# Attention stores one per slot, a weight stream resumed in one go, and two kinds of work moved between engines

## The chip, the cores and the metric

The kernel runs on one core of a Trainium2 chip. The metric is the device time of one launch in microseconds (us). The profile is one further execution, recorded by the hardware profiler; its engines are TensorE (PE, with its weight loads PEld), VectorE (DVE), ScalarE (ACT), GpSimd (POOL) and SyncE (SP), the last of which here issues nearly all transfers between DRAM and the on-chip memory.

## The reference, cut to what matters

The input `x` holds 128 graphs of 64 tokens with 768 features, `adj` a 0/1 matrix per graph. A layer norm and a relu come first, then two attention layers over each graph, then a residual sum:

```python
h = relu(layernorm(x))
for l in range(2):
    m_left, m_right = h @ W_left[l].T, h @ W_right[l].T
    u_left  = einsum('bih,bjh->bij', h, m_left)  / sqrt(768)
    u_right = einsum('bih,bjh->bij', h, m_right) / sqrt(768)
    u = u_left above and on the diagonal, u_right below it      # by triu/tril of adj
    e = exp(u) * adj
    attention = e / (e.sum(-1) + 1e-10)
    ctx = attention @ (h @ W_lin[l].T + b_lin[l])
    h = relu((ctx - mean(ctx)) / (std(ctx, ddof=1) + 1e-3) * a[l] + b[l])
out = x + h
```

## The kernel before, in words

**Passes.** The 8192 tokens are cut into 16 blocks of 512 (8 graphs each), and two blocks make a superblock `U`; there are 8 superblocks. For each layer, `pass_one` (L447) computes the projections m_left and m_right, the scores and the softmax, and stores the attention weights to DRAM (`ATT`). `pass_two` computes the linear layer, applies the attention (`context`) and the norm, and writes the next layer's rows (or the output).

**Products.** A projection is done with a scheme of fast matrix multiplication: `PRODUCTS` lists 29 products, each of a weight tile (a 256x256 block or a sum of blocks, `W_OPS`) and a token tile (a block or a sum, `X_OPS`), whose results are added into the outputs with signs. Each product is made twice, with the left weights (kind 0, into banks X, Y, Z) and the right ones (kind 1, into bank V and two banks `right`), 8 matmuls each, in `project` (L526, the matmul is L538). `read` copies or adds a finished bank into `m`; the additions are DVE's (L221 is the helper `added` that all sums go through). The token sums (`ts`) are GpSimd's. `pass_two`'s `linear` (matmul L1042) uses a similar scheme of 15 products (`ORDER`) over the blocks X, Z, Y, V: its first product writes X, its second (i=1) Z, and its sixth (i=5) is the first to write V.

**Order of the work.** The order is written out by hand. Each product has four slots (0.86 us of PE each), 116 per superblock. `put(slot, f)` hangs work on a slot, `put_all(slot, fs, step)` a list of it, and `run(slot)` (called between matmuls) issues what hangs there. A second list, `idle`, gives up one entry in each slot on which nothing hangs; what is left of it at the end of `pass_one` is issued at once (L763). This decides the order on each engine's queue[...].

**Scores.** The scores of the two blocks of the superblock before are computed after products 0 and 2 (`TURNS`, `scores`, L481, 192 short matmuls). Each block then has a softmax `chain` (L485 to L518): masks times adjacency on GpSimd (`wm`, L489), four DVE reads of the scores' bank (L495), a sum (L499), the exponential on ACT, the normalisation on DVE (L503 to L509), a DVE transpose (L513), and 8 stores to `ATT` (L518). It is a generator; `softmax(u)` is a list of 8 steps of it. The last two blocks have no superblock after them: after the leftover idle work, `pass_one` fills bank X with the bias, computes both scores, the last one's into bank V (L769), runs the chain of block 14 at once, and hangs that of block 15 on slots of `pass_two`.

**Weights.** In the first superblock of layer 0 (`first`, L569) the weight sums are made from the raw weights while the products run: left sums on DVE, right ones (kind "r") on GpSimd for products 2 to 8 and on DVE otherwise (L652). `keep_weight` (L193) stores every product's weights to DRAM (`WS`), and `Singles` hands out the tiles for the sums; a tile is used again once its store has landed. All later superblocks stream the 29 weight pairs from DRAM into a ring of 8 tiles `RING` (`stream`, L196; `wp<-ws` in the profile), the next one being issued after each product (`streamed`, L562). `HELD` (L523) says after which products the stream lags behind: by up to 4 tiles at products 0 and 1, and back by one each at 2, 3, 4 and 5. In `first` the first three streams of the second superblock are issued after product 25 and four more after product 28 (L697 to L702).

**Blocks.** While one superblock is projected, the next one's two blocks are prepared (`block`, L728): `load_rows` (8 loads), `transpose_rows` (L384: in layer 0 the layer norm's statistics and its normalisation on ACT, in both layers four DVE transposes), a `store` of four transfers to `KEPT` (`h<-room`), later `load_h` (`ht<-h`). The statistics of blocks 2 and 3 (`u < 4`) in layer 0 come from ACT passes with an accumulated sum (`sums`); from block 4 on they come from DVE (`mean_var`: two `bn_stats` and a `bn_aggr` per tile).

**Aside.** In superblock 6 of each layer the bias is loaded (`bias`, L780, three loads, each behind a DVE memset in `paced`), in superblock 7 W_lin, whose centring is DVE's and whose 17 sums (`W_SUMS`) are GpSimd's. Both go through `idle`.

Of the kernel before, what the change touches and what calls it, by code (L numbers as in the profile page):

```python
# [17 lines left out]
def kernel(  # L18
# [21 lines left out]
    Q = 4  # L40
# [343 lines left out]
    def transpose_rows(l, u, pool=None):  # L384

        xr, todo = XR[l, u], []
        if l == 0:
            mv = stat.tile([P, Q, 2], F32, name="mv0", bufs=2)
            sd = stat.tile([P, Q], F32, name="sd0", bufs=2)
            rs = stat.tile([P, Q], F32, name="rs0", bufs=2)  # L390
            nb = stat.tile([P, Q], F32, name="nb0", bufs=2)

            def scale():
                nc.scalar.activation(sd, mv[:, :, 1], AF.Sqrt, bias=eps_in)
                nc.vector.reciprocal(rs, sd)
                nc.vector.scalar_tensor_tensor(nb, mv[:, :, 0], -1.0, rs, op0=ALU.mult, op1=ALU.mult)

            def norm(q):
                nc.scalar.activation(xr[q], xr[q], AF.Relu, bias=nb[:, q:q + 1], scale=rs[:, q:q + 1])

            norms = [lambda q=q: norm(q) for q in range(Q)]
            if u < 4:


                xb = blocks_tile(pool)
                total, ss = (stat.tile([P, Q], F32, name=n, bufs=1) for n in ("total", "ss0"))

                def sums(q, to, **how):
                    nc.scalar.activation(xb[:, :, q, :], xr[q].rearrange("p (b j) -> p b j", j=32),
                                         accum_out=to[:, q:q + 1], **how)  # L410

                def inverse():
                    nc.scalar.activation(sd, ss, AF.Sqrt, bias=eps_in, scale=1.0 / H)
                    nc.vector.reciprocal(rs, sd)
                    nc.vector.tensor_mul(nb, total, rs)

                todo.extend([lambda q=q: sums(q, total, func=AF.Copy) for q in range(Q)])
                todo.append(lambda: nc.scalar.mul(total, total, -1.0 / H))
                todo.extend([lambda q=q: sums(q, ss, func=AF.Square, bias=total[:, q:q + 1]) for q in range(Q)])
                todo.extend([inverse, None] + norms)  # L420
            else:
                stats = [lambda q=q: mean_var(mv[:, q, :], [xr[q][:, :HH], xr[q][:, HH:]]) for q in range(Q)]
                for f in stats + [scale] + norms:
                    todo.extend([f, None])
        if l or u >= 4:
            xb = blocks_tile(pool)

        def store():
            to = KEPT[l][u].rearrange("(b i) c t -> i c b t", b=4)
            for a in range(4):  # L430
                nc.sync.dma_start(to[:, :, :, a * P:(a + 1) * P],
                                  xb[a * 32:(a + 1) * 32].rearrange("i (c b) q j -> i c b (q j)", b=4))
# [14 lines left out]
    def pass_one(l, aside):  # L447
        with (tc.tile_pool(name=f"ps_one{l}", bufs=1, space=bass.MemoryType.PSUM) as ps,
# [15 lines left out]
                    nc.sync.dma_start(ADJ[u][h * S:(h + 1) * S].rearrange("p s k i -> p s (k i)"), adj_t[u, h])  # L464

            def softmax(u):
                return [lambda: next(CHAIN[u], None)] * 8

            def scores(u, bank):

# [14 lines left out]
                def chain():  # L485
# [29 lines left out]
                    to = ATT[l][u].rearrange("(b g j) q (h i) -> b h g j q i", b=2, g=2, h=2)  # L515
                    for a in range(4):
                        for g in range(2):
                            nc.sync.dma_start(to[a // 2, a % 2, g], at[a * 32:(a + 1) * 32, g])  # L518

                CHAIN[u] = chain()  # L520

            TURNS = {0: 0, 2: 1}
            HELD = {NP - 2: 1, NP - 1: 2, 0: 3, 1: 4, 2: 3, 3: 2, 4: 1}  # L523
            sent = [(NP if l == 0 else 0) + RINGS - 1]

            def project(U, weights, done):  # L526
                bank, seen, late = {}, (set(), set()), []
# [41 lines left out]
            def first():  # L569
# [2 lines left out]
                ROWS8 = ((0, 0), (0, 2), (1, 1), (1, 3), (0, 1), (0, 3), (1, 0), (1, 2))  # L572
                xs = [ROOM[:, n * H:(n + 1) * H] for n in range(8)]
                pair = lambda n: [RING[n % RINGS][:, k] for k in range(2)]
                early = [s for n in range(3) for s in pair(NP + n)]
                ss = Singles(((20, chunks(2)), (23, chunks(3)), (25, early),
                              (NP, [room(n, 1).rearrange("p (c d) -> p c d", c=K2) for n in range(12, 15)]
                               + [s for n in range(3, RINGS) for s in pair(NP + n)])))
                order = (1, 5, 4, 8, 7, 6, 2, 0, 3)

                def load_x(n):
# [67 lines left out]
                            to, p[:, :3 * P].rearrange("p (c a s) -> p c a s", c=3, a=2))  # L649

                def weight_ops(i, kind):
                    eng = nc.gpsimd if kind == "r" and 2 <= i <= 8 else nc.vector  # L652
                    return [lambda op=op: weight_op(ss, kind, op, eng) for op in W_OPS if op[0] == i]

                stats(0)
# [37 lines left out]
                def done(i):  # L693
                    for kind in "lr":
                        keep_weight(0, ss, kind, i)
                        dead(ss, kind, i)
                    if i == 25:  # L697
                        for n in range(3):
                            stream(0, NP + n)
                    if i == NP - 1:  # L700
                        for n in range(3, RINGS - 1):
                            stream(0, NP + n)  # L702

                return (lambda i, k: ss["lr"[k], PRODUCTS[i][0]]), done
# [17 lines left out]
            for U in range(NU):  # L722
# [4 lines left out]
                if U + 1 < NU:  # L727
                    def block(n, slot):  # L728
                        u = 2 * U + 2 + n
                        *todo, store = transpose_rows(l, u)  # L730
                        slot = put_all(slot, todo)
                        put(slot + 4, store)
                        if u + 1 < NB:
                            put(slot + 5, lambda: load_rows(l, u + 1))
                        slot = max(slot + 13, (92, 104)[n]) if U == 0 and l == 0 else slot + 13
                        put(slot, lambda: load_h(1, l, u))
                        if l:
                            put_all(slot + 22, affine(1, l, u))
# [442 lines left out]
```

## Time and profile before

| what | us |
|---|---|
| time, median of three runs (lowest to highest) | 2750.47 (2747.26 to 2750.59) |
| profiled execution, its own time | 2752.29 |
| its span | 2750.5 |
| PE busy (matmuls) | 2693.7 |
| DVE busy | 1494.2 |
| GpSimd busy | 1365.2 |
| ACT busy | 842.4 |

The three runs lie within 3.3 us of each other. The span is what the profiler saw between the first and the last instruction, 1.8 us less than the time of that execution. Busy times of engines overlap and are not to be added. A line of the timeline gives start, duration, engine, source line, operation, output and inputs, how many in a row, and in brackets the idle time before it with what ended that; SPq is SyncE's queue, on which issues of transfers are listed with the time that the issue took. A line of the waits reads: who waited, for whom, microseconds in all, how often, the longest.

### The profile page before, as it was taken

The numbers are of one execution on the slowest core, as the hardware profiler recorded it, in microseconds if no ns is written. First come the engines' busy times: TensorE is split into PE (matmuls) and PEld (weight loads), VectorE is DVE, ScalarE is ACT, GpSimd is POOL, SyncE is SP. The second block draws the span as 40 slices with busy tenths as digits, with TensorE's granted clock in tenths as the row PEclk, the third lists the DMA queues.
The fourth block names the chain that finished last, engine by engine and source line by source line (L and its number), as shares of the span: only waits on it lengthen the run. The fifth ranks groups of instructions, "written<-read, shape, count | busy, mean of one in ns | idle before, by whom it ended". The sixth has DMA issues, their size and how long they took to land.

```text
span 2750.5 us, 47340 instructions
## 1 busy us (share of the span) xinstructions
PE 2693.7 (98%) x18514; PEld 2315.2 (84%) x18514; DVE 1494.2 (54%) x2445; ACT 842.4 (31%) x1635; POOL 1365.2 (50%) x1060
## 2 busy tenths in 40 slices
PE   9899999999999999999999999999999999999998
PEld 7788888888888888888788888888888888888886
DVE  6645756647547433334344544545446465666667
ACT  5121321321311144445631221211212213544443
POOL 5143344332446676575333424334333285887886
PEclk9999999999999999999999999999999999999999
DMA  7877768768674344558587768767758434555655
GB/s 246 293 230 238 240 216 272 222 196 268 213 279 166 108 130 157 194 154 245 176 282 242 257 206 246 227 219 241 225 173 290 162 138 125 160 169 167 172 164 148
DMA packets 310222, 567.81 MB, mean 206 GB/s; under 512 B 62832, under 2 KB 190064, under 8 KB 301808
## 3 DMA queue, kind: packets, MB, share of 16 engines
q1 hardware_dynamic: 309840, 564.39, 64.5%
q8 instruction: 148, 2.42, 0.4%
q14 instruction: 74, 0.61, 0.1%
q10 hardware_dynamic: 160, 0.39, 0.0%
HBM read 429.40 MB, written 135.27 MB: 205 GB/s over the span
## 4 chain that ended last, share of the span: by engine, by line
PE 93%; DMA 1%; DVE 1%; issue 1%; SPq 1%; ACT 0%; DVEq 0%
PE right L538 17%; PE X L1042 12%; PE X L538 10%; PE V L538 10%; PE Z L538 9%; PE Y L538 8%; PE V L1042 8%; PE Y L1042 6%; PE both L481 5%; PE Z L1042 4%; PE aux L850 2%; PE aux L873 1%; DMA wp<-ws 1%; SPq L368 1%; PE Y L873 0%
## 5 line engine op out<-in xcount | busy, mean ns | idle before, releaser
L221 POOL TENSOR_TENSOR ts<-ht 128x512 f32<-128x512 f32 x352 | 479.9, 1370 | 260.1 <-PE right L538 145.2
L221 POOL TENSOR_TENSOR ts<-ht,ts 128x512 f32<-128x512 f32 x192 | 253.4, 1327 | 480.0 <-PE V L538 255.2
L538 PE MATMUL right<-ts,wp 128*128 128x252 f32 (+1 forms) x1624 | 380.7, 378 | 1.9 <-DVE wp L221 1.9
L538 PEld LDWEIGHTS right<-ts,wp 128*128 128x128 f32 x1624 | 309.7, 191 | 40.6 <-DVE wp L221 2.3
L221 POOL TENSOR_TENSOR ts<-ht,ht 128x512 f32<-128x512 f32 x128 | 164.0, 1290 | 336.8 <-DMA ht<-h 128.7
L221 DVE TENSOR_TENSOR m<-m,X 128x512 f32<-128x512 f32 x160 | 105.6, 685 | 284.4 <-ACT m L303 207.4
L221 DVE TENSOR_TENSOR m<-m,right 128x504 f32<-128x504 f32 (+1 forms) x304 | 200.1, 676 | 95.7 <-PE right L538 83.7
L1042 PE MATMUL X<-room,ts 128*128 128x256 f32 x1024 | 244.2, 380 | 0.2
L538 PE MATMUL Z<-ts,wp 128*128 128x256 f32 x992 | 234.6, 379 | 0.0
L1042 PEld LDWEIGHTS X<-room,ts 128*128 128x128 f32 x1024 | 192.0, 190 | 31.7 <-DVE hl L221 1.8
L538 PEld LDWEIGHTS Z<-ts,wp 128*128 128x128 f32 x992 | 188.7, 190 | 24.5
L538 PE MATMUL X<-ts,wp 128*128 128x256 f32 x864 | 208.5, 385 | 0.2 <-issue 0.2
L538 PE MATMUL V<-ts,wp 128*128 128x252 f32 (+1 forms) x864 | 202.8, 378 | 1.6 <-issue 1.6
L303 ACT ACTIVATE m<-right 128x504 f32<-128x504 f32 (+1 forms) x64 | 36.1, 590 | 520.6 <-PE both L481 500.6
L538 PEld LDWEIGHTS X<-ts,wp 128*128 128x128 f32 x864 | 164.6, 192 | 23.9 <-issue 0.5
L538 PEld LDWEIGHTS V<-ts,wp 128*128 128x128 f32 x864 | 165.2, 191 | 22.7 <-issue 2.0
L1042 PE MATMUL Y<-room,ts 128*128 128x256 f32 x768 | 182.6, 380 | 0.0
L380 ACT ACTIVATE ht<-ht,b_col,a_col 128x512 f32<-128x512 f32 x192 | 140.9, 804 | 101.9 <-DMA ht<-h 101.9
L1042 PEld LDWEIGHTS Y<-room,ts 128*128 128x128 f32 x768 | 146.1, 190 | 20.2 <-issue 0.6
L221 DVE TENSOR_TENSOR m<-m,Y 128x512 f32<-128x512 f32 x144 | 95.8, 684 | 114.8 <-PE Y L538 96.0
L221 POOL TENSOR_TENSOR ts<-ts,ts 128x512 f32<-128x512 f32 x64 | 82.1, 1282 | 152.4 <-PE right L538 135.9
L1008 POOL TENSOR_TENSOR z<-z,b 128x768 f32<-128x768 f32 x62 | 112.8, 1830 | 89.9 <-DVE z L1005 89.9
(215 smaller groups left out, 4817.8 us busy)
## 6 DMA issues: line engine op xcount, KB each, us to landing
wp<-ws SPq DMA_DIRECT2D x435, 512.0 KB, 5.8
ht<-h SPq DMA_DIRECT2D x62, 1536.0 KB, 9.0
h<-room SPq DMA_DIRECT2D x112, 384.0 KB, 6.1
z<-z SPq DMA_DIRECT2D x128, 192.0 KB, 3.2
ws<-wp SPq DMA_DIRECT2D x94, 256.0 KB, 4.3
xr<-in_x_dram SPq DMA_DIRECT2D x120, 192.0 KB, 3.8
out_dram<-xr SPq DMA_DIRECT2D x120, 192.0 KB, 2.7
room<-in_x_dram SPq DMA_DIRECT2D x112, 192.0 KB, 5.2
```

What stands on the lines that cost most here:

```text
L221: (eng.tensor_add if sign == "+" else eng.tensor_sub)(o, a, b)
L303: nc.scalar.activation(to(o), p, AF.Copy, scale=1.0 if sign == "+" else -1.0)
L368: nc.sync.dma_start(t[a * 32:(a + 1) * 32], src.rearrange("(k j) h -> j k h", k=2))
L380: nc.scalar.activation(ht, ht, AF.Relu, bias=cols[1][:, c:c + 1], scale=cols[0][:, c:c + 1])
L481: nc.tensor.matmul(p[h * S + e:h * S + e + 32, q, e:e + 95], ht[:, c, b * S + e:b * S + e + 32], mb[:, e:e + 95], start=(c == 0), stop=(c ...
L538: nc.tensor.matmul(p[:, g], wk[:, c, g * P:(g + 1) * P], tk[:, c, :].rearrange("p (b s) -> p b s", s=S)[:, :, :ns], start=(new and g == c ...
L850: nc.tensor.matmul(cx[k][i, m, :HH], at[j, q, :], hl[j, q, m * HH:(m + 1) * HH], start=True, stop=True)
L873: nc.tensor.matmul(parts[r, k][n][i], at[j, q, :], hl[j, q, cut], start=True, stop=True)
L1008: nc.gpsimd.tensor_add(zs[k], zs[k], rows["b"])
L1042: nc.tensor.matmul(p[:, n], b[t][:, c, r * P:(r + 1) * P], w[s][:, c, :], start=(i in FIRST and i not in PRELOAD and n == c == 0), stop=(c ...
```

## The change

Six edits:

1. Blocks 2 and 3 of layer 0 get their statistics from DVE, as all others do; the list of their steps has 13 entries instead of 19.
2. A chain yields before each of its 8 stores, so it has 16 steps. The first 7 hang on every second slot, the others on one slot each, with the next adjacency load behind them. In layer 0 the second chain starts at slot 78 instead of 82; in superblock 7 at 42 instead of 34, and the adjacency load there at 40 instead of 32.
3. `HELD` loses its entries for products 2, 3 and 4: after product 2 five streams are issued together, and one after each product from there. In `first`, five streams are issued after product 25 and none after product 28.
4. All right weight sums of the first superblock for products beyond 1 are GpSimd's, but those of 12 and 13.
5. A block's store and the next row loads hang two slots later, `load_h` two slots later too, with a floor of slot 103 instead of 104 for block 3; block 3 starts at slot 62 instead of 66.
6. At the end of `pass_one` the last scores go to bank Z instead of V, and three steps of that block's chain run at once; the other 13 hang on slots of `pass_two`.

The diff, cut:

```diff
@@ transpose_rows
-            if u < 4:
-                ...
-                todo.extend([lambda q=q: sums(q, total, func=AF.Copy) for q in range(Q)])
-                todo.append(lambda: nc.scalar.mul(total, total, -1.0 / H))
-                todo.extend([lambda q=q: sums(q, ss, func=AF.Square, bias=total[:, q:q + 1]) for q in range(Q)])
-                todo.extend([inverse, None] + norms)
-            else:
-                stats = [lambda q=q: mean_var(mv[:, q, :], [xr[q][:, :HH], xr[q][:, HH:]]) for q in range(Q)]
-                for f in stats + [scale] + norms:
-                    todo.extend([f, None])
-        if l or u >= 4:
-            xb = blocks_tile(pool)
+            stats = [lambda q=q: mean_var(mv[:, q, :], [xr[q][:, :HH], xr[q][:, HH:]]) for q in range(Q)]
+            for f in stats + [scale] + norms:
+                todo.extend([f] + none * (u >= 4))
+        xb = blocks_tile(pool)
@@ softmax, chain
-                return [lambda: next(CHAIN[u], None)] * 8
+                return [lambda: next(CHAIN[u], None)] * 16
...
                         for g in range(2):
+                            yield
                             nc.sync.dma_start(to[a // 2, a % 2, g], at[a * 32:(a + 1) * 32, g])
...
-            HELD = {NP - 2: 1, NP - 1: 2, 0: 3, 1: 4, 2: 3, 3: 2, 4: 1}
-            sent = [(NP if l == 0 else 0) + RINGS - 1]
+            HELD = {NP - 2: 1, NP - 1: 2, 0: 3, 1: 4}
+            sent = [RINGS - 1 if l else NP + 5]
@@ first
-                early = [s for n in range(3) for s in pair(NP + n)]
+                early = [s for n in range(5) for s in pair(NP + n)]
...
-                               + [s for n in range(3, RINGS) for s in pair(NP + n)])))
+                               + [s for n in range(5, RINGS) for s in pair(NP + n)])))
...
-                    eng = nc.gpsimd if kind == "r" and 2 <= i <= 8 else nc.vector
+                    eng = nc.gpsimd if kind == "r" and i > 1 and i not in (12, 13) else nc.vector
...
-                        for n in range(3):
-                            stream(0, NP + n)
-                    if i == NP - 1:
-                        for n in range(3, RINGS - 1):
+                        for n in range(5):
                             stream(0, NP + n)
@@ pass_one, block and chains
-                        put(slot + 4, store)
+                        put(slot + 6, store)
                         if u + 1 < NB:
-                            put(slot + 5, lambda: load_rows(l, u + 1))
-                        slot = max(slot + 13, (92, 104)[n]) if U == 0 and l == 0 else slot + 13
+                            put(slot + 7, lambda: load_rows(l, u + 1))
+                        slot = max(slot + 15, (92, 103)[n]) if U == 0 and l == 0 else slot + 15
                         put(slot, lambda: load_h(1, l, u))
                         if l:
-                            put_all(slot + 22, affine(1, l, u))
+                            put_all(slot + 20, affine(1, l, u))
...
-                        starts = (6, 56) if U else (26, 66)
+                        starts = (6, 56) if U else (26, 62)
...
-                            put_all(20 + 40 * n if l else 34 + 48 * n, softmax(2 * U - 2 + n) + [lambda n=n: load_adj(2 * U + n)], 2)
+                            steps = softmax(2 * U - 2 + n)
+                            slot = put_all(20 + 40 * n if l else (34, 78)[n], steps[:7], 2)
+                            put_all(slot, steps[7:] + [lambda n=n: load_adj(2 * U + n)])
...
-                        put_all(14 + 20 * n, softmax(2 * U - 2 + n), 2)
-                    put(32, lambda: load_adj(2 * U))
+                        steps = softmax(2 * U - 2 + n)
+                        put_all(put_all(14 + 28 * n, steps[:7], 2), steps[7:])
+                    put(40, lambda: load_adj(2 * U))
@@ end of pass_one
-            scores(NB - 1, ps_st.tile([P, 2 * TH], F32, name="V"))
-            for f in softmax(NB - 2):
+            scores(NB - 1, ps_st.tile([P, 2 * TH], F32, name="Z"))
+            for f in softmax(NB - 2) + softmax(NB - 1)[:3]:
                 f()
-            put_all(2, softmax(NB - 1))
+            put_all(2, softmax(NB - 1)[3:])
```

More of the change, by code (lines that the diff above doesn't have):

```diff
@@ L401, in transpose_rows @@
             norms = [lambda q=q: norm(q) for q in range(Q)]
-            if u < 4:
-                xb = blocks_tile(pool)
[L406 to L415, printed above, removed]
-                todo.extend([lambda q=q: sums(q, total, func=AF.Copy) for q in range(Q)])
-                todo.append(lambda: nc.scalar.mul(total, total, -1.0 / H))
-                todo.extend([lambda q=q: sums(q, ss, func=AF.Square, bias=total[:, q:q + 1]) for q in range(Q)])
-                todo.extend([inverse, None] + norms)
-            else:
-                stats = [lambda q=q: mean_var(mv[:, q, :], [xr[q][:, :HH], xr[q][:, HH:]]) for q in range(Q)]
-                for f in stats + [scale] + norms:
-                    todo.extend([f, None])
-        if l or u >= 4:
-            xb = blocks_tile(pool)
+            stats = [lambda q=q: mean_var(mv[:, q, :], [xr[q][:, :HH], xr[q][:, HH:]]) for q in range(Q)]
+            for f in stats + [scale] + norms:
+                todo.extend([f] + none * (u >= 4))
+        xb = blocks_tile(pool)
         def store():
```

## The prediction

> **What bounds the kernel now.** I read the page first, its busy shares and its chain:
>
> ```profile
> PE 2693.7 (98%) x18514; PEld 2315.2 (84%) x18514; DVE 1494.2 (54%) x2445; ACT 842.4 (31%) x1635; POOL 1365.2 (50%) x1060
> ...
> PE 93%; DMA 1%; DVE 1%; issue 1%; SPq 1%; ACT 0%; DVEq 0%
> ```
>
> TensorE sets the end. The instruction lists of both kernels give PE the same matmuls in the same order (only the bank of one score block differs), so the change can act only on the idle time of PE, about 44 us in 20 gaps, and on the slow clock that follows a gap. Next, PE's waits:
>
> ```profile
> PE both L481 <- issue: 16.9, 7, 3.1
> PE Y L538 <- DMA wp<-ws: 8.0, 2, 5.5
> ...
> PE right L538 <- DVE m L221: 5.6, 1, 5.6
> ...
> PE right L538 <- DVE wp L221: 1.9, 1, 1.9
> ```
>
> Three of them the change touches: the weight stream (8.0), and the two DVE waits, both in the first superblock. The issue waits lie in score blocks, which stay as they are. The most any edit can win there is some 16 us and the slow clock.
>
> [...] after the gaps of 1.9 us and more that fell so, 8 matmuls took 3.4 to 3.7 us instead of 1.89, for 3.4 us; a dip costs up to 1.7 us. [...] DVE adds of 0.69 us take up to 1.75 us (72.58) beside a GpSimd sum. [...] a weight store behind a 1.5 MB store landed after 8.9 us, against a median of 4.3 us for such stores; from 75 to 88 the engines' share is full, 354 GB/s.
>
> **1. The bias stall (gain).** SP's timeline in layer 1, seventh superblock, and PE's:
>
> ```profile
> 2037.93 0.86 SPq L197 DMA_DIRECT2D wp<-ws  x2
> 2059.61 0.33 SPq L778 DMA_DIRECT2D bias<-in_b_lin_dram  x1
> 2060.00 4.62 SPq L431 DMA_DIRECT2D h<-room  x4
> 2064.66 6.26 SPq L368 DMA_DIRECT2D room<-z  x8
> 2071.02 2.07 SPq L197 DMA_DIRECT2D wp<-ws  x4
> ...
> 2077.53 2.90 PE L538 MATMUL Y<-ht,wp 128*128 128x256 f32 x6 [5.50 <-DMA wp<-ws]
> ```
>
> SP issues in order. It stood before the third bias load, then issued a block's store and 8 row loads, and only at 2071.02 the weights of product 9, needed at 2072.03. The new HELD sends five streams after product 2, so in SP's new order those of products 5 to 9 come before that bias load and 10 and 11 before the store. They land by about 2066. Gain: 5.50 plus 1.9 of slow clock = 7.4 us. Late next is product 12, issued about 2071 and needed at 2082, with 6 us to land. If SP stands even longer, the gain falls to 2.
>
> **2. First superblock (layer 0).** Here 16 ACT passes (0.84 to 0.93 us each) become DVE statistics: 1.2 us for each of 8 tiles, 9.6 us, in a stretch where DVE is busy 66.5 of 91 us already (busy times from 40 to 131). In exchange 10 sums (0.69 to 1.4 us) and a negation leave DVE for GpSimd, at 1.27 to 1.7 us each. Block 2's transposes run from about 53.5 instead of 57.3, so the right sum for product 12 is ready at about 62.8 against 63.7: the 1.92 gap shrinks to 1.2 and keeps or loses its slow clock (1.7). Then:
>
> ```profile
> 76.62 0.75 DVE L221 TENSOR_TENSOR wp<-ht,ht 128x512 f32<-128x512 f32 x1
> 87.02 0.69 DVE L221 TENSOR_TENSOR ht<-ht,ht 128x512 f32<-128x512 f32 x1 [9.64 <-DMA ws<-ht]
> ```
>
> The right sum 24 overwrites a tile whose store was issued at 78.03 and landed at 86.93; DVE waited 9.64 us with the accumulations of two products behind it, and PE stood 5.59 us and ran slow for 3.4. After, that sum waits on GpSimd. The store is issued earlier (about 72.5, since DVE and SP reach it sooner) and lands at about 81 with the same 8.9 us. Behind it on GpSimd stand token sums 32 and 33, which product 18 needs at about 82; at 1.27 us each after 81 they are ready at about 84.9: a stall of some 2 to 3 us stays. DVE's new work in block 3 (17 to 20 us in a stretch of 15.5) makes the left sum 27 late, about 93 against 90. Product 21 starts at 96.6 to 98.5 by the first count, against 103.03[...]. Both ends: gain 6.5, loss 1.5; I take a gain of 2.
>
> At the turn to the second superblock a stream wait of 2.46 (130.61): it was issued at 124.27, now with five at about 113, but behind two 1.5 MB loads. It lands near 124.7 against 125. Gain between 0 and 2.5; I take 1.
>
> **3. Attention stores one per slot.** The same 8 stores per block, at 0.55 to 0.6 us of SP each. Spread out they let streams pass; the ring of 8 (27 us of products) hides either order. Price 0. If the ring were empty, 8 stores cost at most 4.8 us of delay per block. ACT's relief is hidden too, ACT being 31% busy. The same answer holds for the moved slots (stores and row loads 2 slots later, the next block's `load_h` 2 later, the second chain at slot 78 instead of 82, in the eighth superblock 42 instead of 34, `load_adj` at 40 instead of 32): 2 slots are 1.7 us and 8 are 6.9, and what they feed is used a whole superblock of 107 us later. What they do to SP's order in layer 1 is counted in step 1, what they do to GpSimd's in step 4. Bound from both sides: one product's stream caught short costs up to the 5.5 us of step 1, none costs 0; I take 0.
>
> **4. The end of each layer's first pass (loss).** Scores of the last block now go to bank Z instead of V, and three steps of its chain run at once. PE's second product of the linear layer (i=1) writes Z; V was needed only at i=5. So a new wait stands there: PE waits until DVE has read the scores from Z, and all of PE is queued behind it. DVE, PE and GpSimd at the end of layer 0:
>
> ```profile
> 906.76 1.41 POOL L489 TENSOR_TENSOR wm<-adj,tri 128x256 f32<-128x256 f32 x2
> ...
> 913.29 2.24 DVE L495 TENSOR_TENSOR wm<-both,wm 32x380 f32<-32x380 f32 x4 [3.08 <-issue]
> 918.32 0.45 DVE L513 STREAM_TRANSPOSE wm<-adj 128x256 f32<-128x256 f32 x1
> 920.13 1.89 PE L1042 MATMUL Z<-room,ts 128*128 128x256 f32 x8
> 923.29 2.23 DVE L495 TENSOR_TENSOR wp<-V,wp 32x380 f32<-32x380 f32 x4
> ```
>
> DVE finishes block NB-2 at 918.77; four reads of Z take 2.24, so Z is free at 921.0 at best, 0.9 after PE wants it. But the chain begins with `wm` on GpSimd, and GpSimd is later after. The eighth superblock's 16 steps per chain fill 32 slots instead of 16, idle work runs only in slots with nothing planned, and 17 sums of W_lin slide to its end. By the new order 30 sums of 1.255 us lie between token sum 38 (ends 877.44) and `wm`, where 21 and a 3.0 us wait lay: 877.4 + 37.7 + 1.4 = 916.5. DVE's chain of 5.5 and the reads of 2.24 follow: 924.25. Stall 4.1, with a dip of 1.7: 5.8. Layer 1:
>
> ```profile
> 2263.73 1.41 POOL L489 TENSOR_TENSOR wm<-adj,tri 128x256 f32<-128x256 f32 x2
> ...
> 2265.83 2.24 DVE L495 TENSOR_TENSOR wm<-both,wm 32x380 f32<-32x380 f32 x4 [2.86 <-POOL wm L489]
> 2271.59 0.45 DVE L513 STREAM_TRANSPOSE wm<-adj 128x256 f32<-128x256 f32 x1
> 2272.80 1.89 PE L1042 MATMUL Z<-room,ts 128*128 128x256 f32 x8
> ```
>
> Here GpSimd sets the chain already. With 30 sums instead of 28 (2.5 us), and 2.7 to 4 us in which the first of them wait for DVE's centring of W_lin, `wm` ends at about 2271; 6.2 of chain and 2.24 of reads give 2279.5. Stall 6.7, dip 1.9: 8.6. Sum over both layers: 14.5 us. The lower end, with GpSimd not behind: 0.9 and 2.2 (2272.04 + 2.24 = 2274.3, less 2272.80 = 1.5, and some clock), 3 us together.
>
> **Sum.** +14.5 − 7.4 − 2 − 1 = +4 us on the profiled run of 2752.3. That run lies 1.8 above the median of 2750.5, where its own noise is of that size; from the median it gives about 2755.
>
> **Rivals.** A, faster: GpSimd keeps up, so the ends cost 3 (the reads of the last scores come right behind the chain), and the first superblock pays its 6.5 and 2.5: +3 − 7.4 − 9 = −13, so 2737; half of that, 2743. For it: DVE's 9.64 wait is gone from DVE for certain. Against: the counts of GpSimd sums ahead of `wm`. B, clearly slower: sum 24's store lands as late as before, at 87. Then GpSimd, with token sums 32 and 33 behind it, holds product 18 until 90.8 against 82.8: about 8 plus a dip of 1.7, where the old 7.3 is given back, so net −1 to +2.5 there, and later sums (28, 35) still short of time give 3 to 5 more; with full ends and a small bias gain the time is 2763. It decides from a landing of about 84 on. C, the score blocks' issue waits (seven, 16.9 us) move: they depend on nothing in the diff that I can name; ±4. D, nothing to measure: HELD's streams arrive in time anyway except once, the ends cost 7 and the gain is 10: 2748.
>
> **Numbers.** Forecast (2750 to 2760) 0.42; A 0.22 (2737 to 2745); B 0.22 (2760 to 2768); D 0.14. A difference under 0.2%, 5.5 us, can't be told from none here. Of the forecast half lies above 2756, so faster 0.22 (A), same 0.21 + 0.14 = 0.35, slower 0.21 + 0.22 = 0.43. Range 2739 to 2768, which takes in B's top and most of A; the likeliest case's own range is 2750 to 2760.
>
> **What would show it.** At 2072 no PE wait for `wp<-ws`. At the ends, `Z L1042` with a wait for DVE, 3 to 5 us in layer 0 and 5 to 8 in layer 1, and `wm` at about 915 and 2270. Near 80, GpSimd waiting for `ws<-ht`, not DVE. Wrong if `wm` isn't late, if the first superblock's end moves by over 7 us, or if a stream wait appears in superblocks where none was.

## The result, and the profile after

The change makes no difference that can be measured: 2747.55 us (median of 18 runs, 2743.23 to 2753.94) against 2747.41 us (18 runs, 2740.97 to 2750.59), ratio 1.0002, 95% interval 0.9994 to 1.0009. That is a balance of gains and losses of some 14 us each, as the traces and the experiments show.

The page of the changed kernel, busy times and chain:

```profile
PE 2687.8 (98%) x18514; PEld 2307.3 (84%) x18514; DVE 1491.3 (54%) x2458; ACT 827.9 (30%) x1601; POOL 1380.3 (50%) x1071
...
PE 91%; POOL 3%; DVE 1%; issue 1%; DMA 0%; SPq 0%; ACT 0%; POOLq 0%; DVEq 0%; ACTq 0%
```

PE still sets the end, but the chain now runs through GpSimd for 3% of the span, where it had none. PE's waits in the changed kernel (who, for whom: us in all, times, longest):

```profile
PE both L460 <- issue: 12.1, 8, 2.8
PE Z L1022 <- DVE wp L474: 6.6, 1, 6.6
PE Z L1022 <- DVE wp L145: 5.3, 1, 5.3
PE V L518 <- POOL wp L221: 3.6, 1, 3.6
PE V L518 <- ACT m L303: 3.0, 1, 3.0
...
PE right L518 <- POOL ht L221: 1.6, 1, 1.6
```

The waits for `wp<-ws` (8.0 us before) and for DVE's `m` (5.6) have gone from this list. Four long ones have come: two for Z, one for a GpSimd sum (`wp`), one for a copy by ACT; with them came short ones for other GpSimd sums (`ht` 1.6, `ts` 1.2 and 0.6).

Both kernels issue the same 18514 matmuls in one order, so the start of the same matmul can be compared in the two traces. In us from one such point to the next, from PE's first matmul on ("to the last score block" means to a matmul inside it):

| stretch | before | after | after − before |
|---|---|---|---|
| to product 8 of the first superblock | 46.1 | 44.1 | −2.0 |
| from there to the second superblock | 87.0 | 88.9 | +1.9 |
| its first four products, with two score blocks | 31.3 | 26.5 | −4.8 |
| on to the last score block of layer 0 | 750.3 | 745.7 | −4.6 |
| from there over the first products of the linear layer | 5.3 | 12.2 | +6.9 |
| second pass, layer 1 up to 1720 us | 796.0 | 795.7 | −0.3 |
| layer 1, 1720 to 1838 us | 121.2 | 116.2 | −5.0 |
| to just behind 2072 us | 255.9 | 248.3 | −7.6 |
| on to the last score block of layer 1 | 171.0 | 171.6 | +0.6 |
| from there over the first products of the linear layer | 8.6 | 16.2 | +7.6 |
| the rest | 464.9 | 465.3 | +0.4 |

The sum is −6.9, although the medians are equal: the execution profiled before (2752.29) lies 4.9 us above its median, the one after (2745.09) 2.5 below. The two ends of the first pass and the stretch at 2072 stand far above such a scatter; the others have to be judged with more profiles.

**The bias stall.** SP's timeline in the seventh superblock of layer 1, changed kernel:

```profile
2026.22 0.33 SPq L758 DMA_DIRECT2D bias<-in_b_lin_dram  x1
2026.65 9.68 SPq L197 DMA_DIRECT2D wp<-ws  x5
2036.42 0.39 SPq L758 DMA_DIRECT2D bias<-in_b_lin_dram  x1
...
2051.79 0.33 SPq L758 DMA_DIRECT2D bias<-in_b_lin_dram  x1
2052.22 0.38 SPq L197 DMA_DIRECT2D wp<-ws  x1
2052.65 6.08 SPq L410 DMA_DIRECT2D h<-room  x4
2058.77 5.05 SPq L368 DMA_DIRECT2D room<-z  x8
2063.96 1.10 SPq L197 DMA_DIRECT2D wp<-ws  x2
```

The five streams now go out between the first and the second bias load, and with the two single ones seven stand before the block's store; PE doesn't wait there.

**The ends of the first pass.** A slow stretch below is one in which the trace's clock record shows PE at a granted clock of 0.50. In the traces of both kernels each lasts 3.41 or 6.83 us, but for the last (8.99 us before, 10.09 after), which reaches the end of the trace. The timeline of GpSimd, DVE and PE at the end of layer 0, changed kernel:

```profile
870.56 16.61 POOL L221 TENSOR_TENSOR room<-room 128x512 f32<-128x512 f32 x13
...
905.68 1.41 POOL L468 TENSOR_TENSOR wm<-adj,tri 128x256 f32<-128x256 f32 x2
...
907.12 2.24 DVE L474 TENSOR_TENSOR wm<-both,wm 32x380 f32<-32x380 f32 x4 [5.43 <-POOL wm L468]
913.73 2.24 DVE L474 TENSOR_TENSOR wp<-Z,wp 32x380 f32<-32x380 f32 x4
...
916.11 3.56 PE L1022 MATMUL Z<-room,ts 128*128 128x256 f32 x8 [5.26 <-DVE wp L145]
```

And in layer 1:

```profile
2253.73 1.42 POOL L468 TENSOR_TENSOR wm<-adj,tri 128x256 f32<-128x256 f32 x2
...
2255.18 2.24 DVE L474 TENSOR_TENSOR wm<-both,wm 32x380 f32<-32x380 f32 x4 [7.73 <-POOL wm L468]
2261.76 2.24 DVE L474 TENSOR_TENSOR wp<-Z,wp 32x380 f32<-32x380 f32 x4
...
2264.15 3.68 PE L1022 MATMUL Z<-room,ts 128*128 128x256 f32 x8 [6.61 <-DVE wp L474]
```

DVE stood idle 5.4 and 7.7 us for `wm`, then needed 6.6 us of chain and 2.24 us for the reads of Z, and PE restarted as they ended. Its 8 matmuls took 3.6 and 3.7 us instead of 1.89: the slow clock comes on top of both waits. `wm` was late because GpSimd had the sums of W_lin still to do: all 17 of layer 0 run between 867.65 and 895.70, 13 of them in one row (first line), and from 865.98 to `wm` GpSimd is idle for no more than 0.1 us at a time.

**The first superblock.** PE's waits there, and the instructions they wait for, changed kernel:

```profile
48.10 0.30 ACT L394 ACTIVATE sd<-mv,eps_in 128x4 f32<-128x4 f32 x1 [4.84 <-DVE mv L339]
...
49.02 3.59 PE L518 MATMUL V<-ht,wp 128*128 128x252 f32 x8 [2.97 <-ACT m L303]
...
81.74 1.55 POOL L221 TENSOR_TENSOR ht<-ht,ht 128x512 f32<-128x512 f32 x1 [12.97 <-PE Y L518]
83.35 1.97 PE L518 MATMUL right<-ht,ht 128*128 128x252 f32 x8 [1.60 <-POOL ht L221]
...
113.27 2.93 POOL L221 TENSOR_TENSOR wp<-wp,wp 128x512 f32<-128x512 f32 x2 [8.26 <-DMA ws<-wp]
114.58 3.73 PE L518 MATMUL V<-ts,wp 128*128 128x252 f32 x8 [3.62 <-POOL wp L221]
```

The square root of block 2's statistics waits on ACT for DVE (4.84 us), with the first copy of V into `m` behind it: the copy starts at 48.30, though the product it copies ended at 44.32. At product 17 the wait is 1.6 us instead of 5.6. For the sum there the profile names PE, whose product ended at 81.75; but the store of the tile landed at 81.58, 0.16 us before the sum began, and in seven other profiles, where the profile names the store, the sum on GpSimd began 0.16 us behind that landing too. So it waited for the store here as well. At product 24 the right sum (29) waits for the store of the tile it is to overwrite. (Expectations below count the first and the last of these waits as products 7 and 25; by the list of products they are 8 and 24.)

### The profile page after: what moved, and what is told of

Read it like the earlier page. It is cut to its first block, busy times and chain, and to the rows that moved or that the text cites. A ratio compares the mean times of both kernels' runs of the same rounds, so it can differ in the third digit from the quotient of the medians.

```text
span 2743.3 us, 47321 instructions
## 1 busy us (share of the span) xinstructions
PE 2687.8 (98%) x18514; PEld 2307.3 (84%) x18514; DVE 1491.3 (54%) x2458; ACT 827.9 (30%) x1601; POOL 1380.3 (50%) x1071
## 4 chain that ended last, share of the span: by engine, by line
PE 91%; POOL 3%; DVE 1%; issue 1%; DMA 0%; SPq 0%; ACT 0%; POOLq 0%; DVEq 0%; ACTq 0%
PE right L518 16%; PE X L1022 12%; PE X L518 10%; PE V L518 10%; PE Y L518 8%; PE Z L518 8%; PE V L1022 8%; PE Y L1022 6%; PE Z L1022 4%; PE both L460 4%; PE aux L830 2%; POOL room L221 1%; POOL ts L221 1%; PE aux L853 1%; PE Y L853 0%
## 5 line engine op out<-in xcount | busy, mean ns | idle before, releaser
L221 DVE TENSOR_TENSOR hl<-hl,V 128x512 f32<-128x512 f32 (+1 forms) x136 | 89.1, 655 | 127.4 <-PE V L1022 119.8
```

The costliest lines, as they stand in the source:

```text
L221: (eng.tensor_add if sign == "+" else eng.tensor_sub)(o, a, b)
```

## Experiments

Theory: the change wins at 2072 us (HELD) and loses at the two ends (bank Z together with a late `wm`), and its first superblock about breaks even. Rivals: the losses hang on other edits, or are only moved when they are taken away; the gain comes from the attention stores. Each ratio is to runs of the kernel before made beside it, with the 95% interval behind it.

**e1: the changed kernel with the sixth edit undone.**

```diff
-            scores(NB - 1, ps_st.tile([P, 2 * TH], F32, name="Z"))
-            for f in softmax(NB - 2) + softmax(NB - 1)[:3]:
+            scores(NB - 1, ps_st.tile([P, 2 * TH], F32, name="V"))
+            for f in softmax(NB - 2):
...
-            put_all(2, softmax(NB - 1)[3:])
+            put_all(2, softmax(NB - 1))
```

> The changed kernel with its sixth edit undone: the last scores go to bank V again, and the whole of the last block's chain hangs on slots of the second pass. Theory (the two new waits of PE for Z cost 6.9 and 7.8 us with their slow clock, and nothing else hangs on them): 14.7 us faster than the changed kernel, so about 2733 us, ratio to the kernel before 0.9948. Rival (the chain of the second-last block ends late anyway, because GpSimd is behind, and PE then waits for V at the sixth product): the wait is only moved, and the time is 2743 to 2747, ratio 0.9985 to 1.0.

2736.14 us, ratio 0.9952 (0.9940 to 0.9964): 0.0050 under the changed kernel's ratio, 13.7 us. The two stretches at the ends took 5.4 and 8.0 us instead of 12.2 and 16.2. The rival has a small part of it: 1.6 us of idle time stand before V in the second pass of layer 1, and the rest of the kernel takes 467.5 us instead of 465.

**e2: the kernel before with HELD alone.**

```diff
-            HELD = {NP - 2: 1, NP - 1: 2, 0: 3, 1: 4, 2: 3, 3: 2, 4: 1}
+            HELD = {NP - 2: 1, NP - 1: 2, 0: 3, 1: 4}
```

> The kernel before with the third edit's HELD alone: five streams go out together after product 2 in every superblock, the first superblock's own streams stay as they were. Theory (the 5.5 us wait at 2072 us and its slow clock go): 7.1 us faster, about 2740 us, ratio 0.9974. Rival (the order of SP's queue in the changed kernel comes from the attention stores and the moved slots, not from HELD): 0 to 2 us faster, ratio 0.999 to 1.0, with the wait for wp<-ws near 2072 still there.

2737.71 us, ratio 0.9962 (0.9950 to 0.9973), a gain of 7.4 to 13.7 us. Of PE's waits for the stream only that at the turn is left:

```profile
PE Y L538 <- DMA wp<-ws: 2.6, 1, 2.6
```

The stretch to behind 2072 took 248.3 us, as in all ten kernels with this HELD; the other four took 255.6 to 256.6. So HELD makes the gain at 2072 alone, with no attention store moved.

**e3: the kernel before with the sixth edit alone** (e1's diff the other way round, on the kernel before).

> The kernel before with the sixth edit alone: the last scores to bank Z, three steps of that chain at once. Theory (the bank alone costs the four reads of 2.24 us behind the chain; the rest of the changed kernel's waits comes from GpSimd being late with wm): PE waits about 0.9 us in layer 0 and 1.5 us in layer 1 for Z, 2.4 us and at most one slow stretch, about 2750 us, ratio 1.0009. Rival (the bank alone makes the whole of it): waits of 5 and 6.6 us, 14.7 us slower, 2762 us, ratio 1.0053.

2750.06 us, ratio 1.0009 (1.0001 to 1.0017), and the waits for Z are short:

```profile
PE Z L1042 <- DVE wp L145: 1.3, 1, 1.3
...
PE Z L1042 <- DVE wp L495: 1.1, 1, 1.1
```

The bank alone costs 2.5 us. The other 11 come from what makes `wm` late, as e5 shows.

**e5: the changed kernel with the old slots of the eighth superblock.** Bank Z stays.

```diff
-                        put_all(put_all(14 + 28 * n, steps[:7], 2), steps[7:])
-                    put(40, lambda: load_adj(2 * U))
+                        slot = put_all(14 + 20 * n, steps[:7], 2)
+                        put(slot, *steps[7:])
+                    put(32, lambda: load_adj(2 * U))
```

> The changed kernel with the eighth superblock's softmax steps back in 8 slots per chain at their old places (the 8 stores of a block in one slot); bank Z and the three early steps stay. Theory (PE's two waits for Z are long because 17 GpSimd sums slid behind the softmax slots and made wm late): the waits fall to about 1.2 us each and 11 us are won against the changed kernel, about 2736 us, ratio 0.996. Rival (GpSimd is late for another reason, such as the token sums of the next superblock): the waits stay at 5 and 6.6 us, ratio 1.000.

2734.71 us, ratio 0.9957 (0.9944 to 0.9971); the waits:

```profile
PE Z L1023 <- DVE wp L145: 1.7, 1, 1.7
PE Z L1023 <- DVE wp L474: 1.6, 1, 1.6
```

So either of the two repairs, another bank or fewer slots, gives back the same 12 to 14 us: the full loss needs both the early reuse of Z and the 17 sums that slid behind the softmax slots. (The waits left are a little longer than the 1.2 us expected.)

**e8: the kernel before with the attention stores and the softmax slots alone** (the second edit, whole; bank V).

> The kernel before with the second edit alone: attention stores one per slot, the moved softmax slots, the old bank V at the end. Theory (the stores are hidden by the ring of weights): no difference beyond 1 us, 2748 us, ratio 1.000. Rival 1 (spread stores let the weight stream through sooner): the wait near 2072 us shrinks too, up to 5 us faster, ratio 0.998. Rival 2 (the later wm makes PE wait for V at the sixth product of the second pass): up to 3 us slower, ratio 1.001.

2746.84 us, ratio 0.9995 (0.9987 to 1.0004). The wait for the stream in layer 1 is as before:

```profile
PE Y L539 <- DMA wp<-ws: 8.0, 2, 5.4
```

Spread stores don't move the stream. Rival 2 is there but small: 1.6 us of idle time stand before V in the second pass of layer 1. They stand there in all six kernels with bank V and the new slots (e1, e6, e7, e8, e9, e12) and in no other.

**e4: the kernel before with what the change does to the first superblock alone** (edit 1, edit 4, the five early streams, the moved slots of that superblock).

> The kernel before with what the change does to the first superblock alone: DVE statistics for blocks 2 and 3, right weight sums on GpSimd, the moved slots of that superblock, five streams after product 25. Theory (the first superblock gives back at products 7 and 25 what it wins at 12 and 17): within 1 us of the kernel before at the start of the second superblock, ratio 0.999 to 1.001. Rival (the gain of 5.3 us at product 17 stays, and the wait of 3.6 us at product 25 belongs to other parts of the change): 4 to 7 us faster, ratio 0.9975 to 0.9985.

2745.57 us, ratio 0.9990 (0.9982 to 0.9998): 0.5 to 4.9 us faster, between the two expectations. From product 8 to the second superblock it took 86.9 us, where kernels with the old first superblock took 86.3 to 87.0 (before, e2, e3, e8): no gain in the place itself. The four products behind it took 26.5 us instead of 30.1 to 32.5. The wait for the copy (2.9 us) and that for GpSimd's `wp` (4.3 in two) stand here too, so they belong to these edits.

**e7: e1 with the square root two slots later.**

```diff
-            for f in stats + [scale] + norms:
+            for f in stats + none * (2 if u == 2 else 0) + [scale] + norms:
```

> As e1, with the square root of block 2's statistics hung two slots later. Theory (PE's wait of about 3 us near 46 us comes from ACT's queue: the square root waits for DVE's last statistics, and the first copy of bank V into m waits behind it): that wait goes with its slow stretch, 3 to 4.4 us there, of which later transposes give back up to 2 at product 12; 2733 to 2735 us, ratio 0.994 to 0.995. Rival (DVE as a whole is late there): the wait stays or moves to product 8, 2736 us or slower.

2733.70 us, ratio 0.9955 (0.9942 to 0.9967), no different from e1. PE's wait for the copy is gone, and another stands at product 12:

```profile
61.73 3.75 PE L518 MATMUL Y<-ts,wp 128*128 128x256 f32 x8 [3.32 <-DVE wp L221]
```

The time is in the theory's range, but the mechanism is the rival's: the wait stays and moves. That DVE is late as a whole, since the statistics come on top of its other work, is the likely reading; no run takes edit 1 alone. The order of ACT's queue only decides where PE notices.

**e6: e1 with block 3's store and the next row loads 8 slots later in the first superblock.**

```diff
-                        put(slot + 6, store)
+                        late = 8 if U == 0 and l == 0 and n else 0
+                        put(slot + 6 + late, store)
                         if u + 1 < NB:
-                            put(slot + 7, lambda: load_rows(l, u + 1))
+                            put(slot + 7 + late, lambda: load_rows(l, u + 1))
```

> The changed kernel with bank V at the end (as in e1), and in the first superblock the store of block 3 and the row loads of block 4 hang 8 slots later, about where they were before. Theory (these 12 transfers hold SP for 10.8 us in front of the weight stores whose landing the right sums 29 and 31 wait for): PE's wait for V on GpSimd's wp near 111 us (3.4 us, and two slow stretches) goes, 5 to 7 us faster than e1, about 2730 us, ratio 0.993. Rival (the sums are late because GpSimd or the tiles of the five early streams hold them): the wait stays, 2736 us, ratio 0.995.

2731.59 us, ratio 0.9948 (0.9934 to 0.9962); it is the fastest median of all, but its interval overlaps e1's. The wait has moved to a later such sum, at product 26, in GpSimd's and PE's timeline:

```profile
103.75 2.96 POOL L221 TENSOR_TENSOR wp<-wp,wp 128x512 f32<-128x512 f32 x2
118.72 1.26 POOL L221 TENSOR_TENSOR wp<-room,wp 128x512 f32<-128x512 f32 x1 [12.01 <-DMA ws<-wp]
...
120.03 3.44 PE L518 MATMUL V<-ht,wp 128*128 128x252 f32 x8 [3.43 <-POOL wp L221]
```

SP's order decides when these stores land, but a wait of the same length stays.

**e9: e1 with the first superblock's streams as before** (three after product 25, four after 28; three pairs of tiles that sums may use until product 25, not five).

```diff
-                early = [s for n in range(5) for s in pair(NP + n)]
+                early = [s for n in range(3) for s in pair(NP + n)]
...
                     if i == 25:
-                        for n in range(5):
+                        for n in range(3):
+                            stream(0, NP + n)
+                    if i == NP - 1:
+                        for n in range(3, RINGS - 1):
                             stream(0, NP + n)
```

> As e1, with the first superblock's streams as before: three after product 25, four after product 28, and so three pairs of ring tiles for the sums that end by then instead of five. Theory (the right sums of products 24 to 26 wait for stores because they were given tiles whose stores land late, a matter of the tiles handed out): PE's waits for GpSimd's wp go, and the wait of 2.5 us for the stream at the turn comes back; 2 to 4 us faster than e1, 2732 to 2734 us, ratio 0.994. Rival (SP reaches these stores late whichever tiles are used): the waits stay and the turn's wait comes on top, 2738 to 2740 us, ratio 0.9965.

2735.28 us, ratio 0.9952 (0.9939 to 0.9966). PE doesn't wait for GpSimd's `wp` at all, and the turn's wait is back:

```profile
133.20 1.97 PE L518 MATMUL Y<-ht,wp 128*128 128x256 f32 x8 [2.40 <-DMA wp<-ws]
```

So the tiles handed out are the cause of the wait at product 24: five pairs promised to early streams leave fewer tiles for the last sums, and these get one whose store is late. The streams themselves can't be: in the changed kernel they went out at 119.84, behind that wait. e12 and e11 below agree, with the tiles open to these sums and no wait there. The times of e9 and e1 are the same; the gain that was expected doesn't show: one wait is traded for the other, and other waits vary by as much.

**e12: e1 with the five streams after product 27 and their tiles open to sums until then.**

```diff
-                ss = Singles(((20, chunks(2)), (23, chunks(3)), (25, early),
+                ss = Singles(((20, chunks(2)), (23, chunks(3)), (27, early),
...
-                    if i == 25:
+                    if i == 27:
```

> As e1, with the five early streams after product 27 instead of 25, and so their ring tiles open to sums that end by product 27. Theory (SP reaches these streams at about 120 us anyway, since it stands before the stores ahead of them, so nothing is lost at the turn; and the right sums of products 24 to 26 get tiles without a late store): both PE's wait for V near 111 us and the wait at the turn are gone or under 1 us; 4 to 6 us faster than e1, 2730 to 2732 us, ratio 0.9935. Rival (the streams go out later by the two products, 6.9 us): the turn's wait is 2 to 4 us, 2733 to 2736 us, ratio 0.995.

2739.70 us, ratio 0.9971 (0.9961 to 0.9981), some 4 us slower than e1, though the two intervals just touch. The sums don't wait any more, but the streams went out at 131.5 us in place of 120.5, behind the stores of their own tiles, and PE waited:

```profile
134.81 3.50 PE L518 MATMUL Y<-ht,wp 128*128 128x256 f32 x8 [7.55 <-DMA wp<-ws]
```

The rival holds in kind, with more than the 2 to 4 us and a longer time than the 2733 to 2736 us it named.

**e10: e2 with one right sum more on GpSimd, that of product 17.**

```diff
-                    eng = nc.gpsimd if kind == "r" and 2 <= i <= 8 else nc.vector
+                    eng = nc.gpsimd if kind == "r" and (2 <= i <= 8 or i == 17) else nc.vector
```

> The kernel before with HELD as in e2, and of the right sums only the one of product 17 (sum 24) moved to GpSimd. Theory (this one sum makes DVE wait 9.6 us, and everything behind it): PE's 5.6 us wait near 83 us falls to about 1.6, 5 us with its slow clock; 2732 to 2734 us, ratio 0.9945. Rival (the store lands when it lands, and product 17 or 18 waits as long on GpSimd): as e2, 2738 us, ratio 0.996.

2736.06 us, ratio 0.9960 (0.9948 to 0.9973): as e2.

```profile
82.80 1.26 POOL L221 TENSOR_TENSOR ht<-ht,ht 128x512 f32<-128x512 f32 x1 [27.19 <-DMA ws<-ht]
...
84.11 3.73 PE L538 MATMUL right<-ht,ht 128*128 128x252 f32 x8 [6.99 <-POOL ht L221]
```

PE waits 7 us for the sum on GpSimd as it did for the product sums behind it on DVE (6.9 in e2). The store lands when it lands.

**e11: e2 with all right sums on GpSimd that the change puts there.**

> The kernel before with HELD as in e2 and all the right sums on GpSimd that the change puts there, the statistics still on ACT and the slots as before. Theory (the other moved sums relieve nothing that PE waits for, and 29 to 31 wait on GpSimd as they would on DVE): as e10 within 1.5 us, about 2733 us. Rival 1 (GpSimd holds the late sums and PE waits for them near product 25, as in e1): 2736 to 2739 us. Rival 2 (a lighter DVE ends its waits at products 12 and 21 too): 2729 to 2731 us.

2736.42 us, ratio 0.9965 (0.9952 to 0.9977): as e2 and e10, with the same wait, 6.75 us for the sum at product 17. But the wait at product 12 is gone, as rival 2 had it, and the wait near product 25 that rival 1 named is not there. From product 8 to the second superblock e10 took 84.6 us and e11 82.9, against 86.3 in e2 and 88.9 in the changed kernel. These are single profiles, and the medians don't show such a gain, since their intervals overlap e2's; but they point to the moved sums (edit 4) as the useful part there, and to the statistics and the five early pairs as what takes it back.

**The balance.** One edit each, on the kernel before: HELD −10.4 us (0.9962), first superblock −2.7 (0.9990), stores and slots −1.4 (0.9995). The sixth edit on top of these is 13.7 (1.0002 less 0.9952). The sum is −0.8; the change as a whole measured +0.5. The parts add up within their intervals. One part was not run by itself: the later slots for stores, row loads and `load_h` outside the first superblock (edit 5); the sum leaves about 1 us for it. The versions that keep HELD and avoid the late Z (e1, e5, e6, e7, e9) are all 0.43 to 0.52% faster than the kernel before, which the changed kernel equals; between them the runs don't decide. e12 gains 0.29%, since it pays at the turn.

## Why the prediction was right, and where it was not

**Step 1, the bias stall: right.** Forecast −7.4; the aligned traces show −7.6 over the stretch, and e2 alone 7.4 to 13.7. Product 12, named as late next, caused no wait. The 3 us that e2's median has beyond the forecast are inside its interval.

**Step 4, the ends: right in mechanism and size.** Thirty GpSimd sums were counted ahead of `wm` in each layer, and thirty stand there in the trace. Forecast 5.8 and 8.6 us, 14.5 together; the traces show 6.9 and 7.6, e1 13.7. `wm` was forecast to end at 916.5 on the time scale of the kernel before. It ended at 907.1, with PE 9.5 us ahead by then (score block at 906.6 instead of 916.1), which makes 916.6. In layer 1 it ended at 2255.15 with PE 14.9 ahead, 2270.0 against the forecast 2271. The lower end of that step, GpSimd not behind, was put at 3 us: e3 measured 2.5.

**Step 2, the first superblock: the gain of 2 is within e4's interval, but it isn't made as told.** Three of its terms failed: product 8 and product 24, which it put at nothing, and the gain at product 17. The wait at product 12 was to shrink to 1.2 us; it went altogether, because PE had already been held up at product 8: the square root on ACT's queue, with the copy of V behind it, was not priced (2.97 us and a slow stretch); e7 shows that the wait comes back at product 12 when that queue is freed. At product 17 the step that PE would still wait 2 to 3 us was right (1.60, and 0.62 and 0.58 for the token sums behind), and the store was issued at 72.8 and landed at about 81.6, forecast 72.5 and 81, with the same 8.8 us from issue to landing. But the gain there is smaller than it looks: in three other profiles with the old first superblock and the sum on DVE (e2, e3, e8) the matmuls of product 17 started again at 85.4 to 86.3, and the 88.35 of the profile before was the latest of its kind; against 83.35 that leaves 2 to 3 us. And the wait at product 24 (3.62 us and 6.8 us of slow clock) was not foreseen: I followed the queues but not which tiles `Singles` would give to the last sums. In its own place the superblock wins nothing (88.9 us against 86.3 to 87.0, in e1 89.0, in e5 89.4); what e4 won it won behind the turn. The loss of 1.5 at this step's other end was the author's estimate for DVE sums that run beside GpSimd sums (up to 1.75 us for one in the trace before, 0.69 alone); what they cost the superblock no run shows.

**The turn: right by luck.** Streams were to go out at 113 and land at 124.7; they went out from 119.84 on, the first landed at 129.34, and PE, held up at product 24, came later too and started the second superblock at 133.07, as before (133.06).

**Step 3, the stores: right.** Forecast 0; e8 measured −1.4, interval −3.6 to +1.1.

**Rival C was under-sized and counted for nothing.** The waits that the profile calls issue, most of them in score blocks (18.9 and 13.3 us), sum to 23.1 us before and 15.9 after; 4 us were allowed for them. They vary from profile to profile, but not only by chance: in the stretch behind the turn the eight kernels with the new statistics and slots in the first superblock took 25.7 to 28.6 us, the six with the old ones 30.1 to 32.5. The time forecast lay 4.5 us above the median it started from and the measured change is 0.5; most of that distance fits these waits, but no run isolates them. By the runs of single edits it lies in HELD (10.4 us where 7.4 were counted), in the stores and slots (1.4 where 0 was) and in the ends (13.7 for 14.5), each within the interval of its run.

**Readings.** Slow stretches followed some of the gaps of PE and not others: in the kernel before one of 1.92 us at 63.67 brought a stretch of 3.41 us in the clock record and one of 2.46 us at 133.06 none; what decides it was not shown. And 1.7 us isn't the most that such a dip costs: behind the wait at product 24 the clock was halved for 6.83 us, nearly all of it with PE at work. PE's waits before are 22, not 20. The median landing of 4.3 us is that of the stores `ws<-wp`; those from `ht`, to which the one at 78.03 belongs, have 4.9. The two ends add up to 14.4, not 14.5. None of these changes the forecast.

**Rival B** didn't occur: the store landed at 81.6, before the 84 from which it decides. e10 shows the wait it describes where the slots are the old ones: PE stood 7 us for GpSimd, since it came to product 17 earlier, though the store landed at 82.6. **Rival A** needed GpSimd to keep up, which e3 and e5 show is possible but this change prevents.

The time is inside the range of 2739 to 2768 us, which took in most of the cases, and just outside the 2750 to 2760 of the likeliest case, which was some 4 us too slow. 2748 was rival D's number, but not by its reasons: it had the ends at 7 us and the gains at 10, and the runs show some 14 of each. The steps hold; that the gains cancel the losses to within half a us was not foreseen, and is chance.

## What to carry to other kernels

A wait that is removed is worth what the next one leaves of it, so look for the condition under it: in the first superblock each repair left the same wait or met another (e10 and e11 the same store at product 17, e6 a store at product 26, e7 a late sum on DVE, e9 and e12 the stream at the turn), whereas the stream order at 2072 and the bank at the ends had nothing late behind them and gave their whole 7 to 14 us. When a helper list runs only in free slots, count what new entries push out of it: here 16 added softmax slots in one superblock delayed an unrelated GpSimd operation, measured against PE's last score block, by 8 us in one layer and 5 in the other, and with the early reuse of a bank cost PE 11. One profile is one draw (here 4.9 us above its median); align the same instructions over several kernels' traces before a difference of 2 us is given a cause.

## What was not expected of the hardware

The issue waits, most of them in score blocks, for which the profile names no releaser, depend on what else is going on: they sum to 14.9 to 19.6 us in the seven profiles built on the changed kernel and 19.9 to 24.2 in the other seven, built on the kernel before. A single one, at the same matmuls near 580 us, ranged from 0.81 us (e12) to 2.52 us (e11). In the six profiles where it was 2.24 us or longer, a slow stretch of 3.41 us began within 1.3 us of its end; in the eight where it was 1.94 us or shorter, none did.

The traces' records of transfers show what these waits end with. One of the two queues of instructions on the page, q8, carries 148 transfers of 16 KB in each of the 14 profiles. Of the 159 issue waits of PE longer than 0.3 us in all profiles, 153 ended 2.2 to 2.9 us after the start of such a transfer and 1.1 to 1.6 us after its end. In the kernel before, for example, the wait that ended at 160.62 follows a transfer from 158.35 to 159.31. The transfers are 18.6 us apart on average, so chance would put about one wait in 25 there. The other six are the 1.6 us before V in the second pass. So in score blocks PE very likely waits for its own next instructions. An estimate from the same numbers fits this: if all 148 transfers serve PE's 18514 matmuls and 18514 weight loads, each brings some 250 of them. A score block uses 384 in 4.06 us, so 250 last 2.6 us there, about as long as one transfer takes to act; between other products 32 take 3.45 us, and 250 last 27. No run tested it, by moving the score blocks against the instruction stream or by making them smaller.

Why the transfers start earlier in some kernels, and which edit shortens the waits, was not settled: the stretch behind the turn goes with the first superblock's edits, the one at 1720 to 1838 us was 115.6 to 117.2 us in all ten kernels with the new HELD and 117.7 to 122.6 in the four without.
